# A decoder layer with sixteen experts on one core: the fifth product of the experts' output with 128 rows, and another place for the first expert's up products

## The chip, the core and the metric

The program runs on one core of one Trainium2 chip. A core has a tensor engine (PE; its weight loads are listed apart as PEld), a vector engine (DVE), a scalar engine (ACT), GpSimd (POOL), and SyncE (SP), which here only issues transfers. Each engine works through its own instructions in a fixed order and waits at an instruction until the semaphores named in it have been reached. The metric is the device time of one execution in microseconds (us); lower is better.

## The reference

The layer is: layer norm, self-attention with 4-bit weights, layer norm, cross-attention over a compressed context, layer norm, and a mixture of 16 experts, each part added to `x`. Tokens: 16 x 64 = 1024 of width 256. Only the experts matter for this change:

```
scores = softmax(xt @ Wg.T)                      # 1024 x 16
...                                              # top 4 of the 16, limited to 2 of 4 groups
h = silu(einsum('td,eid->eti', xt, W1)) * einsum('td,eid->eti', xt, W3)   # inner width 176
expert_out = einsum('eti,edi->etd', h, W2)
y = einsum('etd,te->td', expert_out, combine)
z = (silu(xt @ Ws1.T) * (xt @ Ws3.T)) @ Ws2.T    # shared expert, width 352
return y + z
```

## The kernel before

**Precision.** The products of the experts are done in `fp32r`, a format coarser than float32. To keep accuracy each operand is split into a high part (a rounded copy, made on ACT) and a low part (what the rounding left, a subtraction on DVE or POOL); `parts_of` (L111) does it for activations and `weight_parts` (L268) for an expert's weights. A product is then high by high, high by low, and low by high: three matmuls in place of one.

**An expert's inner width is 176 = 128 + 48.** The first 128 make one block of `h` with its high part `h_p[0]` and low part `h_p[1]`. The other 48 (filled up with zeros to 64) make a second block. Its high and its low part share one tile, `h_p[2]`: rows 0 to 63 hold the high part, rows 64 to 127 the low part. The second block of the down weights, `w2[1]`, has the same 64 rows twice, once in each half. So one matmul of 128 rows, `(h[2], w2[1][0])`, gives high by high and low by high at once. What remains of that block is high by the weights' low part, `(h[2][:64], w2[1][1][:64])`, a matmul of 64 rows. `expert_output` (L291) is thus five matmuls into one stretch of PSUM, of which the fifth has 64 rows.

**Who calls it.** `send_outputs` (L1273) calls it three times for each of the 15 routed experts (384 slots in three blocks of 128). `dense_out` (L1098) and `dense_output` (L1321) call it for the sixteenth expert, which is computed for all tokens: four times each.

**The routed experts.** Each token's rows are scattered by POOL's indirect transfers into `xd`, a table in device memory with 384 slots for each expert (`send`, L820; a token's k-th choice is sent with the k-th round of sends). `expert_inputs` (L1233) loads an expert's 384 rows (`xr`, issued by SP; the load waits for the rounds of sends that may hold rows of it), turns them with six PE transposes, and splits them (`xs`). `expert_weights` (L1222) loads its weights (640 KB, issued by SP), rounds them on ACT (L270) and subtracts on DVE, or on DVE and POOL (L275). `expert_hidden` (L1255) does 18 up matmuls into three PSUM tiles, then silu, product and splitting on ACT and DVE; it leaves its last up matmul in `up_done[0]`. `send_outputs` does the three times five down matmuls, copies the results out of PSUM (L1281) and scatters them back with three indirect transfers (L1286). At the end `load_outputs` fetches them and `add_outputs` (L1309) adds them with their weights.

**Order.** The loop at L1335 works on three experts at a time: in step `e` it asks for the inputs and weights of expert `e`, the hidden part of expert `e-1`, and the outputs of expert `e-2`. The text of the program does not give the order alone: a scheduler in the framework orders the instructions of each engine by its own estimate, and `tc.issue_after(ins)` tells it to place what follows behind an instruction. In step 2 the hidden part of expert 1 comes ahead of the inputs of expert 2, which are placed behind `up_done[0]`; in all other steps inputs come first. The raw weights (`w`) have two buffers, their parts three, `xr` three.

Of the kernel before, what the change touches and what calls it, by code (L numbers as in the profile page):

```python
# [42 lines left out]
E, INTER, NGRP, TOPK, TOPKG = 16, 176, 4, 4, 2  # L43
# [28 lines left out]
def decoder_layer(ctx: ExitStack, tc: tile.TileContext, a: dict, out: bass.AP):  # L72
# [29 lines left out]
    def matmuls(ps, pairs):  # L102
        for n, (l, r) in enumerate(pairs):
            m = nc.tensor.matmul(ps, lhsT=l, rhs=r, start=(n == 0), stop=(n == len(pairs) - 1))  # L104
        return m.ins
# [184 lines left out]

    def expert_output(ps, w, h_p, cols):  # L291

        w2 = [[p[:, W_UP + k * D : W_UP + (k + 1) * D] for p in w] for k in range(2)]
        h = [p[:, cols] for p in h_p]
        return matmuls(
            ps,
            [
                (h[0], w2[0][0]),
                (h[0], w2[0][1]),
                (h[1], w2[0][0]),  # L300
                (h[2], w2[1][0]),
                (h[2][:64], w2[1][1][:64]),
            ],
        )

    with ExitStack() as attn:
# [528 lines left out]
        def slots_are_short():  # L835

            ps = av_tile()[:, :E]
            nc.tensor.matmul(ps, lhsT=ones, rhs=before[:, NI, :], start=True, stop=True)
            most = fs.tile([128, 1], F32, tag="most", name="most")
            nc.vector.tensor_reduce(most, ps[:, : E - 1], AX.X, ALU.max)  # L840
            short = fs.tile([128, 1], I32, tag="short", name="short")
            nc.vector.tensor_scalar(short, most, SLOTS + 0.5, None, ALU.is_gt)
            return nc.values_load(short[:1], min_val=0, max_val=1)
# [98 lines left out]
        with (  # L942
# [155 lines left out]
            def dense_out(h_p, half, tiles, add):  # L1098
                for k in tiles:
                    ps = av_tile()[:, :D]  # L1100
                    expert_output(ps, w_last, h_p, slice(k * 128, k * 128 + 128))
                    add(half, k, ps)
# [117 lines left out]
    gated, up_done = [None], [None]  # L1220

    def expert_weights(src, down_lo=nc.gpsimd):  # L1222
        return weight_parts(
            src,
            fw.tile([128, W_COLS], F32, tag="w123", name="w123"),
            [
                fw.tile([128, W_COLS], F32R, tag=f"w123{n}", name=f"w123{n}", bufs=3)
                for n in range(2)
            ],
            down_lo,  # L1230
        )

    def expert_inputs(e):  # L1233

        t = fx.tile([128, SLOTS // 128, ROW], F32, tag="xr", name="xr", bufs=3)
        first = TOPK * NT + (E - 2 - e) * SLOTS
        load = nc.sync.dma_start(
            out=t, in_=xd[first : first + SLOTS].rearrange("(b p) d -> p b d", p=128)
        ).ins
        for k in range(min(TOPK, e + 1)):  # L1240
            behind(load, sent_for[k])
        to = fx.tile([128, SLOTS // 128], U32, tag="to", name="to", bufs=4)
        parts = [fx.tile([128, 2, SLOTS], F32R, tag=f"xs{n}", name=f"xs{n}") for n in range(2)]
        for c in range(2):
            ps = at_tile([128, 512])[:, :SLOTS]
            for b in range(SLOTS // 128):
                nc.tensor.transpose(
                    ps[:, b * 128 : (b + 1) * 128], t[:, b, c * 128 : (c + 1) * 128], ident
                )
            lows.append(parts_of(ps, parts[0][:, c, :], parts[1][:, c, :]))  # L1250
        with tc.issue_after(lows[-1]):
            nc.vector.tensor_copy(to, t[:, :, D + e])
        return parts, to

    def expert_hidden(w, xs, n):  # L1255


        ps, up_done[0] = expert_up(w, xs, n)
        g, h, g2, h2 = (
            fh.tile([128, SLOTS], F32, tag=tag, name=tag)[:, :n] for tag in ("g", "h", "g2", "h2")  # L1260
        )
        h_p = [
            fh.tile([128, SLOTS], F32R, tag=tag, name=tag)[:, :n] for tag in ("hp0", "hp1", "hp2")
        ]
        nc.scalar.activation(g, ps[0], AF.Silu)
        nc.vector.tensor_tensor(h, ps[1], g, ALU.mult)
        parts_of(h, h_p[0], h_p[1])
        silus.append(nc.scalar.activation(g2[64:], ps[2][:64], AF.Silu).ins)
        nc.vector.tensor_tensor(h2[:64], ps[2][64:], g2[64:], ALU.mult)
        gated[0] = parts_of(h2[:64], h_p[2][:64], h_p[2][64:])  # L1270
        return h_p

    def send_outputs(e, w, h_p, to):  # L1273
        last = []
        y = fy.tile([128, SLOTS // 128, D], F32, tag="y", name="y")
        ps = [av_tile() for _ in range(2)]
        for b in range(SLOTS // 128):
            cols = slice(b * 128, (b + 1) * 128)
            last.append(expert_output(ps[b // 2][:, b % 2 * D : (b % 2 + 1) * D], w, h_p, cols))
            last.append(  # L1280
                (nc.vector.tensor_copy if b == 1 and e < E - 3 else nc.scalar.copy)(  # L1281
                    y[:, b, :], ps[b // 2][:, b % 2 * D : (b % 2 + 1) * D]
                ).ins
            )
        for b in range(SLOTS // 128):
            sent = nc.gpsimd.indirect_dma_start(  # L1286
                out=yd[: (E - 1) * SLOTS + min(TOPK, E - 1 - e) * NT],
                out_offset=bass.IndirectOffsetOnAxis(ap=to[:, b : b + 1], axis=0),
                in_=y[:, b, :],
                in_offset=None,  # L1290
            ).ins
            side_by_side(sent, returned)
            last.append(sent)
        return last

    def load_outputs(k):

        tiles = []
        for n in range(NI // 2):
            t = fy.tile([128, 2, D], F32, tag="got", name="got", bufs=9)  # L1300
            first = (E - 1) * SLOTS + (TOPK - 1 - k) * NT + n * 256
            got = nc.sync.dma_start(
                out=t, in_=yd[first : first + 256].rearrange("(i p) d -> p i d", p=128)
            ).ins
            behind(got, returned)
            tiles.append(t)
        return tiles
# [10 lines left out]
    def dense_hidden(w, half, n):  # L1318
        return expert_hidden(w, [p[:, :, n * 256 : n * 256 + 256] for p in normed[half]], 256)

    def dense_output(w, h_p, half, n, add):  # L1321
        for b in range(2):
            ps = av_tile()[:, :D]
            expert_output(ps, w, h_p, slice(b * 128, b * 128 + 128))
            add(half, 2 * n + b, ps)
# [7 lines left out]
    with tc.issue_after(lows[-1]), tc.issue_after(silus[-1]):  # L1333
        ws[0] = expert_weights(a["W123"][0], nc.vector)
    for e in range(E + 1):  # L1335
        if e == 2:

            low = lows[-1]
            hs[e - 1] = expert_hidden(ws[e - 1], xs[e - 1][0], SLOTS)
        if e < E - 1:  # L1340
            low = lows[-1]
            with tc.issue_after(up_done[0] if e == 2 else low):
                xs[e] = expert_inputs(e)
            if e >= 1:
                with tc.issue_after(low), tc.issue_after(silus[-1]):
                    ws[e] = expert_weights(a["W123"][e], nc.vector if e < 3 else nc.gpsimd)
        if 0 <= e - 1 < E - 1 and e != 2:
            hs[e - 1] = expert_hidden(ws[e - 1], xs[e - 1][0], SLOTS)
        if e - 2 >= 0:
            if e == E:  # L1350

                with tc.issue_after(gated[0]):
                    h_p = dense_hidden(w_last, 1, 0)
            last = send_outputs(e - 2, ws.pop(e - 2), hs.pop(e - 2), xs.pop(e - 2)[1])
            if e - 2 == E - TOPK - 2:
                short = slots_are_short()
            if e == 6:
                with tc.issue_after(gated[0]), tc.issue_after(silus[-1]):
                    routed.append(weights_of_choices(1))
            k = e - 2 - (E - 1 - TOPK)  # L1360
            if k >= 0:
                got[k] = load_outputs(k)
# [135 lines left out]
```

## Time and profile before

| what | value |
|---|---|
| median of 3 runs | 598.12 us (594.16, 598.12, 598.73) |
| the profiled execution | 594.01 us, span from first to last instruction 592.2 us |
| mean granted PE clock | 0.973 |
| self-attention and the start | 0 to about 220 us |
| cross-attention and routing | about 220 to 459 us |
| routed experts | about 459 to 574 us |
| last additions and stores | about 574 to 592 us |

A group line of the profile reads: line, engine, operation, output<-input, rows*columns of the array that are used, the shape, the count; then busy time and the mean duration of one in ns; then idle time before it, and what ended the idle time. The duration of a matmul includes the depth of the pipeline: matmuls overlap, so what one costs the engine is the distance from its start to the start of the next. In the timeline like instructions in a row are merged into one line, with the start of the first, the length of all, and their number. The windows view gives each engine's busy time in a stretch, the granted PE clock (1.00 is full), and the share of time in which the DMA engines were busy.

### The profile page before, as it was taken

To read this page: it belongs to the slowest core of one execution; us is meant where nothing else is said; L and a number is where in the kernel's file an instruction comes from. 1 tells how busy PE (TensorE), PEld (TensorE's weight loads), DVE (VectorE), ACT (ScalarE), POOL (GpSimd) and SP (SyncE) were. 2 spreads that over 40 slices of the span, in tenths; PEclk is the share of its full clock that TensorE was granted. 3 is DMA by queue.
4 is the path that set the end of the run, shared out by engine and by line. 5 is a ranking of instruction groups with operands and counts; after the bars stand their busy time and mean duration, and the time that the engine had idled before them with its cause. 6 is when DMAs were issued, how large, how long until landed. Compare 5 with 4: busy or idle time off the path is not lost.

```text
span 592.2 us, 10572 instructions
## 1 busy us (share of the span) xinstructions
PE 558.4 (94%) x3999; PEld 452.9 (76%) x3999; DVE 403.4 (68%) x879; ACT 280.6 (47%) x524; POOL 232.5 (39%) x213
## 2 busy tenths in 40 slices
PE   5989999999999989999999999999989799999992
PEld 5878988988889875757777577576778688888871
DVE  5454636554465789847668487789648587888766
ACT  3657574575665432221431332333435276867551
POOL 4192000010000004526334454442545546768773
PEclk8989999999999999999999999999989799999996
DMA  8667042141300499481020000000413677565275
GB/s 247 159 195 208 25 136 91 53 143 50 95 1 1 137 265 293 128 243 30 1 70 1 8 1 1 28 2 26 165 69 95 231 225 239 176 228 184 100 252 184
DMA packets 56293, 70.82 MB, mean 120 GB/s; under 512 B 13872, under 2 KB 42768, under 8 KB 56240
## 3 DMA queue, kind: packets, MB, share of 16 engines
q1 hardware_dynamic: 51408, 58.71, 33.5%
q0 software_dynamic: 3696, 10.36, 4.6%
q10 hardware_dynamic: 1136, 1.05, 0.5%
q8 instruction: 32, 0.52, 0.4%
q14 instruction: 21, 0.17, 0.1%
HBM read 48.61 MB, written 21.86 MB: 119 GB/s over the span
## 4 chain that ended last, share of the span: by engine, by line


## 5 line engine op out<-in xcount | busy, mean ns | idle before, releaser
L973 POOL TENSOR_TENSOR roped<-rt,rt 128x512 f32<-128x512 f32 x48 | 62.7, 1328 | 82.8 <-DVE rt L967 80.5
L967 DVE TENSOR_TENSOR rt<-mm,rope_q 128x512 f32<-128x512 f32 x96 | 61.5, 684 | 23.7 <-PE mm L104 23.1
L104 PE MATMUL mm<-xn,w_q 128*128 128x512 f32 x288 | 74.2, 403 | 0.5 <-ACT xn L214 0.5
L104 PEld LDWEIGHTS mm<-xn,w_q 128*128 128x128 f32 x288 | 52.1, 188 | 14.4 <-issue 2.7
L1286 POOL DMA_INDIRECT yd<-y,to x45 | 49.4, 1099 | 34.7 <-DVE y L1281 13.5
L104 PE MATMUL mm<-xs,w 128*128 128x384 f32 x270 | 57.0, 358 | 1.2 <-ACT w L270 0.6
L104 PEld LDWEIGHTS mm<-xs,w 128*128 128x128 f32 x270 | 48.0, 196 | 4.4 <-DVE w L275 0.8
L318 ACT ACTIVATE p<-p 128x512 f32<-128x512 f32 x32 | 20.2, 630 | 65.7 <-DVE p L317 65.7
L513 POOL TENSOR_TENSOR wo<-code,scale 128x512 fp32r<-128x512 f32 x8 | 10.6, 1330 | 102.1 <-PE mm L104 94.1
L988 PE MATMUL mm<-roped,w_s 128*64 128x512 f32 x192 | 46.3, 601 | 0.0
L104 PE MATMUL av<-w,hp 128*128 128x256 f32 (+1 forms) x225 | 45.8, 314 | 0.1
L605 DVE TENSOR_TENSOR x<-mm,x 128x256 f32<-128x256 f32 x64 | 26.0, 419 | 29.1 <-PE mm L104 27.9
L104 PEld LDWEIGHTS av<-w,hp 128*128 128x128 f32 (+1 forms) x225 | 33.9, 187 | 9.0 <-issue 0.7
L104 PE MATMUL mm<-wo,o 128*128 128x256 f32 x256 | 39.5, 295 | 0.1
L104 PE MATMUL mm<-wv,xn 128*128 128x256 f32 x256 | 36.0, 292 | 1.4 <-ACT kT L550 1.4
L315 DVE TENSOR_REDUCE sm_m<-at 128x8 f32<-128x512 f32 x32 | 21.7, 679 | 21.8 <-PE at L565 20.9
L104 PE MATMUL mm<-xn,wq 128*128 128x512 f32 x128 | 35.4, 413 | 0.4 <-ACT xn L214 0.4
L104 PE MATMUL mm<-xn,wk 128*128 128x512 f32 x128 | 35.4, 407 | 0.0
L582 PE MATMUL av<-pt,v 128*128 128x128 f32 x256 | 34.5, 277 | 0.0
L104 PEld LDWEIGHTS mm<-wv,xn 128*128 128x128 f32 x256 | 32.5, 193 | 2.5 <-ACT kT L550 1.6
L104 PEld LDWEIGHTS mm<-wo,o 128*128 128x128 f32 x256 | 32.9, 190 | 1.5 <-issue 0.4
L582 PEld LDWEIGHTS av<-pt,v 128*128 128x128 f32 x256 | 32.0, 191 | 1.2
(216 smaller groups left out, 1150.1 us busy)
## 6 DMA issues: line engine op xcount, KB each, us to landing
w<-in_W SPq DMA_DIRECT2D x15, 640.0 KB
code<-in_codes SPq DMA_DIRECT2D x32, 256.0 KB
scale<-in_scales SPq DMA_DIRECT2D x32, 256.0 KB
xr<-xd SPq DMA_DIRECT2D x15, 408.0 KB
xd<-zeros SPq DMA_DIRECT2D x8, 720.0 KB
yd<-zeros SPq DMA_DIRECT2D x8, 512.0 KB
got<-yd SPq DMA_DIRECT2D x16, 256.0 KB
wq<-in_Wq SPq DMA_DIRECT2D x4, 512.0 KB
```

Source lines behind the costliest of these rows:

```text
L104: m = nc.tensor.matmul(ps, lhsT=l, rhs=r, start=(n == 0), stop=(n == len(pairs) - 1))
L315: nc.vector.tensor_reduce(m, sc, AX.X, ALU.max)
L318: exps.append(nc.scalar.activation(p, p, AF.Exp, scale=scale).ins)
L513: mults[n] = eng.tensor_tensor(w, *loaded[gr].pop(n), ALU.mult).ins
L582: nc.tensor.matmul(av[:, k * 128 : (k + 1) * 128], lhsT=v[:, i, k0 : k0 + HD], rhs=pt[:, i].rearrange("p a q -> p (a q)"), start=True, sto ...
L605: nc.vector.tensor_tensor(x[i], ps, x[i], ALU.add)
L967: nc.vector.tensor_tensor(mt, ps3, rope_table(t, 2 * ab + k), ALU.mult)
L973: nc.gpsimd.tensor_tensor(r.rearrange("p (b s) -> p b s", s=S), one, two, op)
L988: nc.tensor.matmul(ps[h // 2][(h % 2) * 64 : (h % 2) * 64 + 64], lhsT=w_s[:, t, blk, ab, :], rhs=roped[2 * t + ab], start=first[h], stop=l ...
L1286: sent = nc.gpsimd.indirect_dma_start(out=yd[: (E - 1) * SLOTS + min(TOPK, E - 1 - e) * NT], out_offset=bass.IndirectOffsetOnAxis(ap=to[:, ...
```

## The change

Two edits. In `expert_output` the fifth matmul takes all 128 rows of `h_p[2]` and of the weights' low part; with it the product of low by low, which was left out before, comes in for the second block. In the loop the arrangement of step 2 is used in step 1 as well: the hidden part of expert 0 comes ahead of the inputs of expert 1, which are placed behind its last up matmul, and ahead of the weights of expert 1.

```diff
@@ expert_output
                 (h[0], w2[0][1]),
                 (h[1], w2[0][0]),
                 (h[2], w2[1][0]),
-                (h[2][:64], w2[1][1][:64]),
+                (h[2], w2[1][1]),
@@ the loop over the experts
     for e in range(E + 1):
-        if e == 2:
+        if e in (1, 2):
             low = lows[-1]
             hs[e - 1] = expert_hidden(ws[e - 1], xs[e - 1][0], SLOTS)
         if e < E - 1:
             low = lows[-1]
-            with tc.issue_after(up_done[0] if e == 2 else low):
+            with tc.issue_after(up_done[0] if e in (1, 2) else low):
                 xs[e] = expert_inputs(e)
...
-        if 0 <= e - 1 < E - 1 and e != 2:
+        if 0 <= e - 1 < E - 1 and e > 2:
             hs[e - 1] = expert_hidden(ws[e - 1], xs[e - 1][0], SLOTS)
```

In the built program this moves instructions on four engines between the end of the shared expert and the first outputs of expert 1. PE does the 18 up matmuls of expert 0 without a break; before, the six transposes of expert 1 stood after the third and the twelfth of them. On ACT the rounding of expert 1's weights (L270) comes behind the two silus of expert 0 instead of ahead of the shared expert's last pieces; on DVE the two subtractions for those weights come behind the two products (L1266, L1269) of expert 0. On SP the first three loads (`xr` of experts 0 and 1, weights of expert 2) stay; the weights of expert 3 are asked for behind `xr` of experts 2 and 3 instead of ahead of them. POOL's order stays as it was. Two of the four output blocks in `dense_out` also come 10 matmuls or so later on PE.

## The prediction

> **What bounds the kernel now.** I read the page first (which engine is full), then the groups by shape for the stretch from 380 us on, then PE's timeline to see single starts, then the windows for clock and load, and last the queues of SP and POOL. The view of the chain of waits holds nothing for this run, so what ends last is read from PE's own gaps. The page, and the windows of the expert stage:
>
> ```profile
> PE 558.4 (94%) x3999; PEld 452.9 (76%) x3999; DVE 403.4 (68%) x879; ACT 280.6 (47%) x524; POOL 232.5 (39%) x213
> ...
> 474.00:574.00 100.00, 98.89 (x578) 85.70 (x578) 80.23 (x150) 67.30 (x137) 67.29 (x57) 1.00 0.61 200
> ```
>
> From 474 to 574 us (columns PE, PEld, DVE, ACT, POOL, clock, DMA share, GB/s) PE has work at all times but 1.1 us; DVE is busy 80 us, ACT and POOL 67. So PE's pitch sets this stage, with DVE next. The groups by shape:
>
> ```profile
> L104 PE MATMUL av<-w,hp 128*128 128x256 f32 x180 | 32.9, 297 | 0.1
> L104 PE MATMUL av<-w,hp 64*128 64x256 f32 x45 | 17.2, 381 | 0.0
> L104 PE MATMUL mm<-ws,sh 96*128 96x256 f32 x24 | 3.8, 281 | 0.0
> ```
>
> The 45 fifth products (64 rows) last 381 ns each, their 128-row neighbours 297, products of the same width with 96 rows 281. Durations overlap, so I take starts. The timeline, asked from later and later points inside one group of five (a merged line starts with the first matmul still running):
>
> ```profile
> 487.38 0.94 PE L104 MATMUL av<-w,hp 128*128 128x256 f32 x5
> ...
> 487.50 0.83 PE L104 MATMUL av<-w,hp 128*128 128x256 f32 x4
> ...
> 487.62 0.71 PE L104 MATMUL av<-w,hp 128*128 128x256 f32 x3
> ...
> 487.73 0.59 PE L104 MATMUL av<-w,hp 128*128 128x256 f32 x2
> ...
> 487.94 0.38 PE L104 MATMUL av<-w,hp 64*128 64x256 f32 x1
> 488.25 0.97 PE L104 MATMUL mm<-xs,w 128*128 128x384 f32 x4
> ```
>
> The first four start 0.12 us apart, the 64-row one 0.21 after its forerunner, and the next instruction 0.31 after it. The group takes 488.25 - 487.38 = 0.87 us where five steps of 0.117 would be 0.585: 0.285 us too much. The start of the stage:
>
> ```profile
> 456.35 3.38 PE L104 MATMUL mm<-ws,sh 128*128 128x256 f32 x27
> ...
> 460.63 0.79 PE L104 MATMUL mm<-xs,w 128*128 128x384 f32 x3 [0.24 <-ACT xs L112]
> 465.50 0.87 PE L1247 MATMUL at<-ident,xr 128*128 128x128 f32 x3 [4.09 <-DMA xr<-xd]
> 466.03 3.23 PE L104 MATMUL mm<-xs,w 128*128 128x384 f32 x9
> ...
> 455.20 6.38 SPq L1237 DMA_DIRECT2D xr<-xd  x2
> 461.74 2.34 SPq L269 DMA_DIRECT2D w<-in_W  x2
> 470.25 4.21 SPq L1237 DMA_DIRECT2D xr<-xd  x3
> ...
> 468.00:469.00 1.00, 1.00 (x4) 0.96 (x4) 0.00 (x0) 0.00 (x0) 0.94 (x1) 0.50 1.01 411
> ```
>
> PE stands 4.09 us at expert 1's transposes until its rows land, and then runs at clock 0.50: windows of 1 us show 0.50 from 465 to 471 and 0.75 in 471 to 472. The nine products at 466.03 need 3.02 us (469.05 - 466.03), 0.335 each; at full clock 18 of them need 3.25 (546.87 to 550.12), 0.18 each.
>
> **The change part by part. (a) The fifth product.** It occurs 15 x 3 = 45 times in the routed experts and 4 + 4 times for the sixteenth. Each saves 0.285 us of PE if it then steps like its 128-row neighbours: 12.8 us for the 45. The bounds: 0 and 0.285 each. Against it stands the Trainium skill, "TensorE: Matmul & The Clock Gate", Part 3 and "Why this matters for your kernels": a single matmul of 32 rows takes the same time as one of 128, so rows below 128 gain by concurrency alone. By that rule 64 or 128 rows are one price and (a) is worth nothing. The rows decide: the shared expert mixes 96-row and 128-row products, and 27 of them start (3.38 - 0.28) / 26 = 0.119 us apart, so neither fewer rows nor the end of a group costs; only the 64-row kind does, on both its sides. I take 0.285. By the rule the sum below would lose its larger term.
>
> What of the 12.8 lies on the path: from 474 to 574 PE would need 87 us, DVE still 80, and POOL 67 plus 45 gaps of 0.30 that follow its indirect transfers, 81. They hide nothing now (they have 20 us to spare), but after the saving they have 7 and will make PE wait at times. One row prices that: in 510 to 530 us DVE is busy 17.13 of 20 and PE loses 0.9 of 20. At DVE 92% I allow 3% to 4% of 87 us, 3.2 us. So (a) brings 9.6 there, between 4 (DVE and POOL take most) and 12.8. The four blocks of `dense_out` lie ahead of the wait for expert 1's rows, which they only lengthen; the four at the end lie beside DVE's additions (PE waits 1.3 to 1.7 us for DVE there): nothing for both. If DVE were faster those at the end would bring 1.1.
>
> **(b) Expert 0's up products ahead of expert 1's rows.** Moved forward: 18 matmuls, two silus, two roundings, four DVE operations. Put behind them: six transposes, two roundings, two subtractions and the slot copy of expert 1, and the rounding (1.26 us) and two subtractions (1.55) of its weights. The wait itself stays: expert 1's load keeps its place on SP, second of these, behind the same sends, and lands at about 465.5. But 15 of the 18 products now run inside it: from 461.4, held a little by DVE's low parts (ready at about 462.1), to about 464.2. That takes 15 x 0.18 = 2.7 us out of the time after 465.5. PE then stands only 1.3 us (2.4 with the four shorter `dense_out` blocks ahead).
>
> The clock: 465.5 to about 471.5 ran at half, so 3.0 us of work were lost. The skill's page on the clock gate (Part 1, "What's actually happening") says the clock falls after one idle window of about 3.4 us and that windows run freely. By it a stand of 1.3 to 2.4 us leaves the clock at 1.00 and (b) brings 2.7 + 3.0 = 5.7; without it, if any stand of over a microsecond lowered the clock, 2.7. The nearest rows (a stand of 4.09 fell, stands under 0.6 us in 474 to 574 did not) leave it open; I take the full clock.
>
> Given back: ACT rounds expert 1's weights after the second silu, at about 464.6 to 465.9, so DVE's chain from there is 1.55 (weights) + 0.5 + 0.56 + 0.5 + 0.16 + 0.56 = 3.8, until about 469.7; the 18 up products of expert 1 then end at about 470.4 instead of 474.7, a gain of 4.3. Next late: `xr` of expert 3 waits for the last round of sends (POOL ends it at 470.2) and lands at about 474.5, where PE now wants it at about 474; and the weights of expert 3 are queued on SP behind that load. They were issued at 463.7; now at about 472.5, land 2 to 4 us later (640 KB at the 300 GB/s that the DMA engines reach there) and need 1.26 us on ACT: 477 to 478, where PE wants them at about 477.5. That is 0 to 1 us. Less DMA traffic at 464 to 469 (share 1.0 now) helps expert 1's and 2's rows by as much again at best. I take 4.0 for (b), between 0.5 (clock falls, late weights) and 6.
>
> **Sum.** 594.0 - 9.6 - 4.0 = 580.4 for an execution like the profiled one. It lies 4.1 under the median of the runs shown, which by the same sum goes to 584.5. I say 583, since I can't tell which kind of run will be in the middle.
>
> **The rivals.** *DVE and POOL become the bound.* For: 80 and 81 us of work in a stage of 87, with chains between them; a DVE operation of 0.56 us lasts far longer beside POOL's subtraction:
>
> ```profile
> 539.41 1.95 DVE L113 TENSOR_TENSOR hp<-h,hp 128x384 fp32r<-128x384 f32 x1
> ...
> 539.64 1.29 POOL L275 TENSOR_TENSOR w<-w,w 128x512 fp32r<-128x512 f32 x1
> ```
>
> Against: DVE idles 20 of 100 us now. Then (a) brings 4 to 5 and (b) 3: about 590 on the median.
>
> *The price is not of the 64 rows* but of whatever stands fifth. Against: the 96-row groups above close without it, and the price falls on both sides. Then (b) alone: about 594.
>
> *Slower: more collisions of DVE with POOL.* An expert takes 6.73 us now (up products at 540.13 and 546.87), DVE about 5.5 of it. A collision like the one shown adds 1.4. A tighter PE moves DVE's splitting under POOL's subtraction more often. Two more per expert would make DVE need 8.3 and cost 15 x 1.6 = 24, less 4 from (b): about 618; it decides from 1.2 + 0.3 = 1.5 us more per expert on. Against: the subtraction runs once per expert, 1.3 to 2.0 us long, and one collision per expert is there already.
>
> **How the numbers follow.** What a measurement of this kernel can tell from no change is about 1%, 6 us. Chances: the forecast 0.71 (576 to 590), DVE and POOL as the bound 0.18 (587 to 594, four fifths of it faster by over 1%), the price elsewhere 0.07 (592 to 597), slower 0.04. Faster 0.71 + 0.14 + 0.01 = 0.86, same 0.10, slower 0.04. Range: from 575 (594.0 with all of 12.8 and 6) to 592, which takes in most of the first rival.
>
> **What would show it.** No 64*128 row is left; the fifth product starts 0.12 after the fourth and the next 0.12 to 0.18 after it; an expert's pitch falls from 6.73 to 6.0 to 6.2; DVE's share from 474 on rises to about 90%. PE's wait for expert 1's rows is under 2.5 us, and no 0.50 shows after 464 us. The prediction is wrong if a 128-row fifth product keeps the 0.3 us behind it, if the pitch stays above 6.5 with PE waiting for DVE or POOL, or if a new PE wait of over 2 us stands ahead of expert 2's transposes or expert 3's first product.

## The result, and the profile after

The changed kernel takes 589.94 us, the kernel before 594.30 (medians of 18 runs each, 586.70 to 593.14 and 590.03 to 598.73): a ratio of 0.992, 95% interval 0.9895 to 0.9944. About 4.4 us came, where the prediction had 13.6. The profiled execution took 590.21 us, with a span of 588.4 and a mean granted clock of 0.979. Ratios here and below leave out executions more than 1.5% slower than the fastest of their kernel (a single one of 1042 us, of the kernel with 128 rows only, among them), while the medians take in all. From L293 on, line numbers are higher by one than before.

The page's row of busy time, and the window from 474 to 574 us (columns PE, PEld, DVE, ACT, POOL, clock, DMA share, GB/s), of the changed kernel:

```profile
PE 540.4 (92%) x3999; PEld 444.3 (76%) x3999; DVE 401.0 (68%) x879; ACT 279.4 (47%) x524; POOL 230.1 (39%) x213
...
474.00:574.00 100.00, 83.94 (x567) 79.78 (x566) 80.10 (x152) 64.50 (x134) 70.88 (x60) 1.00 0.66 217
```

PE was busy 98.89 of these 100 us before and is busy 83.94 now. Not all of this is saved work: the routed products now end 6.5 us sooner, and the window takes in a stand of 4.89 us behind them (the last line below). What became of the saving shows in the steady experts further down. The group of down products, and the timeline around one group of five:

```profile
L104 PE MATMUL av<-w,hp 128*128 128x256 f32 x225 | 35.1, 289 | 4.0 <-DVE y L1282 3.3 <-DVE most L841 0.5 <-ACT y L1282 0.3
...
505.84 0.75 PE L104 MATMUL av<-w,hp 128*128 128x256 f32 x5
506.43 0.49 PE L1248 MATMUL at<-ident,xr 128*128 128x128 f32 x3
...
573.75 0.77 PE L104 MATMUL av<-w_last,hp 128*128 128x256 f32 x2 [4.89 <-DVE x L936]
```

All 225 products now have 128 rows, and five of them with what follows take 506.43 - 505.84 = 0.59 us, where it was 0.87. At its source the saving is what the prediction said. The end of the group line shows a first price: PE waits 3.3 us for DVE's copy `y` out of PSUM, where these products had 0.1 us of idle time in all before.

To compare kernels I cut the steady part out: from the first up product of expert 5 to that of expert 13, eight experts. It runs from 498.20 to 553.90 us before and from 496.20 to 549.30 after. The windows of the two kernels, in this order:

```profile
498.20:553.90 55.70, 54.68 (x315) 47.37 (x314) 46.77 (x89) 38.70 (x76) 39.62 (x32) 1.00 0.61 200
```

```profile
496.20:549.30 53.10, 47.27 (x317) 45.08 (x316) 46.99 (x90) 38.75 (x78) 41.10 (x34) 1.00 0.67 221
```

PE's busy time falls by 7.4 us, 0.93 an expert; the time by 2.6, 0.33 an expert. DVE is busy for the same 47 us in both, which is now 88% of the time. What PE waits for in the same windows, before and then after (us in total, times, longest):

```profile
PE mm L104 <- ACT w L270: 0.6, 1, 0.6
PE mm L104 <- DVE w L275: 0.2, 1, 0.2
```

```profile
PE mm L104 <- ACT w L270: 2.8, 4, 1.4
PE mm L104 <- DVE w L275: 1.7, 2, 1.3
PE av L104 <- DVE y L1282: 0.8, 1, 0.8
PE av L104 <- DVE most L841: 0.5, 1, 0.5
```

0.8 us of waiting became 5.8. So two thirds of what was saved on PE turned into standing. The largest part, 2.8 us, is for ACT's rounding of the weights. The copy `y` has only 0.8 here; 2.46 of its 3.3 us fall in one wait at the start of the stage (shown further down). ACT's rounding itself waits 0.5 us in this window, for PE, and never for a load, so the loads of weights don't hold these experts. How such a wait comes about shows in the timeline of the changed kernel:

```profile
514.62 1.68 DVE L1253 CAST to<-xr 128x3 uint32<-128x3 f32 x1
514.98 1.28 POOL L275 TENSOR_TENSOR w<-w,w 128x512 fp32r<-128x512 f32 x1
516.21 0.41 DVE L1282 COPY y<-av 128x256 f32<-128x256 f32 x1
516.68 0.85 PE L104 MATMUL av<-w,hp 128*128 128x256 f32 x5 [0.84 <-DVE y L1282]
516.87 0.94 DVE L275 TENSOR_TENSOR w<-w,w 128x768 fp32r<-128x768 f32 x1
517.87 1.66 PE L104 MATMUL mm<-xs,w 128*128 128x384 f32 x8 [0.34 <-DVE w L275]
518.32 1.10 ACT L112 CAST hp<-h 128x384 fp32r<-128x384 f32 x2 [2.31 <-DVE h L1267]
```

DVE's copy of 3 slot numbers a row takes 0.16 us elsewhere. Here it lasts 1.68 and ends at 516.30, with POOL's subtraction (514.98 + 1.28 = 516.26). Behind it in DVE's queue stand `y`, which PE wants for the next down products, DVE's part of the weights, which PE wants for the next up products, and `h`, which ACT stands 2.31 us for.

### The profile page after: what moved, and what is told of

The parts are those of the page before. It is cut to its first block, busy times and chain, and to the rows that moved or that the text cites. A ratio compares the mean times of both kernels' runs of the same rounds, so it can differ in the third digit from the quotient of the medians.

```text
span 588.4 us, 10571 instructions
## 1 busy us (share of the span) xinstructions
PE 540.4 (92%) x3999; PEld 444.3 (76%) x3999; DVE 401.0 (68%) x879; ACT 279.4 (47%) x524; POOL 230.1 (39%) x213
## 4 chain that ended last, share of the span: by engine, by line
PE 71%; DVE 12%; DMA 6%; ACT 4%; issue 4%; POOL 2%; SPq 0%; DVEq 0%; ACTq 0%; POOLq 0%
PE mm L104 42%; PE mm L989 6%; PE av L583 5%; PE at L566 4%; DMA yd<-y,to 4%; PE at L335 3%; PE at L1012 2%; PE av L1025 2%; PE av L104 2%; PE mm L431 2%; ACT w L270 2%; DVE rt L968 1%; DVE w L275 1%; DMA w<-in_W 1%; DVE x L1317 1%
## 5 line engine op out<-in xcount | busy, mean ns | idle before, releaser
L104 PE MATMUL mm<-xs,w 128*128 128x384 f32 x270 | 54.5, 344 | 8.3 <-ACT w L270 3.2
L104 PEld LDWEIGHTS mm<-xs,w 128*128 128x128 f32 x270 | 45.8, 188 | 11.5 <-ACT w L270 4.2
L104 PE MATMUL av<-w,hp 128*128 128x256 f32 x225 | 35.1, 289 | 4.0 <-DVE y L1282 3.3
L104 PEld LDWEIGHTS av<-w,hp 128*128 128x128 f32 x225 | 30.5, 188 | 5.7 <-DVE y L1282 3.9
```

## The experiments

A series is a set of runs of several kernels on one chip, with the kernel before among them; "again" in the table is another series. "First sends" below is the first of POOL's last sixteen scatters of rows (448.05 us in the profile before; sixteen others, of the first half of the tokens, go out from 411.67 on). It is the reference point because it moves by itself: up to it all these kernels run the same instructions in the same order, and yet it came between 445.28 and 453.86 us in their profiles. "Expert n" is its first up product after that, "end" the end of the span after that; the pitch is from expert 4 to expert 14, divided by ten. All are read from the timelines, one profile a row. A pitch says little of a kernel whose expert 4 comes early and whose expert 5 does not.

| kernel | ratio to before (95%) | expert 0 | expert 1 | expert 4 | pitch | end |
|---|---|---|---|---|---|---|
| before | 1 | 12.6 | 23.5 | 43.5 | 6.85 | 144.2 |
| changed | 0.992 (0.9895 to 0.9944) | 11.6 | 18.1 | 43.3 | 6.48 | 141.1 |
| changed, again | 0.9908 (0.9883 to 0.9934) | 11.6 | 18.1 | 43.0 | 6.49 | 140.4 |
| 128 rows only | 0.996 (0.9938 to 0.9982) | 15.8 | 22.5 | 43.2 | 6.48 | 140.5 |
| 128 rows only, again | 0.9892 (0.9856 to 0.9928) | 11.8 | 22.0 | 41.2 | 6.54 | 139.4 |
| reordering only | 1.0187 (1.0146 to 1.0229) | 22.1 | 29.2 | 50.9 | 6.86 | 152.5 |
| reordering only, again | 0.9994 (0.9977 to 1.0011) | 12.5 | 19.0 | 41.5 | 6.85 | 142.2 |
| reordering only, third | 0.9992 (0.9974 to 1.0011) | 12.5 | 19.1 | 42.8 | 6.85 | 143.9 |
| before, low parts on DVE | 0.9932 (0.9908 to 0.9955) | 12.6 | 22.3 | 43.1 | 6.68 | 142.3 |
| 128 rows, low parts on DVE | 0.9803 (0.976 to 0.9846) | 11.6 | 22.5 | 40.5 | 6.25 | 134.8 |
| the same, again | 0.9827 (0.9788 to 0.9866) | 11.6 | 22.4 | 40.5 | 6.03 | 132.4 |
| changed, low parts on DVE | 0.9841 (0.9773 to 0.991) | 15.1 | 22.6 | 42.3 | 6.04 | 135.4 |
| the same, again | 0.9824 (0.9784 to 0.9865) | 11.8 | 18.0 | 38.2 | 6.21 | 132.1 |
| changed, weights of 1 early | 0.9998 (0.9971 to 1.0025) | 15.2 | 24.9 | 46.8 | 6.60 | 147.3 |
| the same, again | 0.9921 (0.9885 to 0.9956) | 11.6 | 17.5 | 40.4 | 6.48 | 138.3 |

**The parts alone.** The kernel before with the 128-row product, where no instruction changes its place on any engine:

```
-                (h[2][:64], w2[1][1][:64]),
+                (h[2], w2[1][1]),
```

> The kernel before with only the fifth product at 128 rows; every engine keeps its order. Theory A (VectorE is the next bound): each group of five takes 0.59 us instead of 0.87, but an expert's pitch from 500 us on falls by only about 0.3 us and VectorE has almost no idle time there: ratio 0.990 to 0.996 (3 to 6 us). Rival B (the fifth product alone brings what the sum said, 9 us or more, and the reordering takes it back): ratio 0.985 or less.

593.67 us, 0.996: the upper edge of the first theory. On another chip:

> The kernel before with the 128-row fifth product alone, once more. Theory A (the steady experts lose 0.375 us each, some 4 us over ten experts and 5 with the others, of which the end gives 1 back; the first runs fell on a chip where the start of the stage was late): ratio 0.989 to 0.994, pitch 6.47 to 6.48 us. Rival B (it is worth no more than the first runs said): 0.994 to 0.998.

586.49 us against 593.18 of the kernel before on that chip, 0.9892. That chip also ran the changed kernel again (below) at 589.03. So the gain of the change is in this one line, and no gain of the reordering on top of it shows. The two series differ by more in whole times (gains of 2.6 and 6.7 us) than from the first sends to the end of the span (140.5 and 139.4 us, against 144.2 before and 141.1 and 140.4 for the changed kernel). The reordering in the kernel before:

```
-        if e == 2:
+        if e in (1, 2):
...
-            with tc.issue_after(up_done[0] if e == 2 else low):
+            with tc.issue_after(up_done[0] if e in (1, 2) else low):
...
-        if 0 <= e - 1 < E - 1 and e != 2:
+        if 0 <= e - 1 < E - 1 and e > 2:
```

> The kernel before with only the reordering of step 1; the fifth product keeps 64 rows. Theory A: the stand for expert 1's rows shrinks, but the weights of expert 3 are loaded late and ScalarE stands for them about 4 to 5 us, so expert 4's up products start within 1 us of before: ratio 0.997 to 1.002. Rival B: the reordering costs more than it brings: ratio 1.005 or more. Rival C: it brings the 4 us of the sum: 0.993 or less.

606.91 us, a loss of 11: the first rival's case. The table says where: expert 0 starts 22.1 us after the first sends, where before it was 12.6, and after that nothing is lost. Ahead of expert 0 the edit changes no more than the order of a few groups of the shared expert and of `dense_out`, and the rounding and subtraction of weights between them. Windows of this run:

```profile
464.00:468.00 4.00, 1.03 (x8) 0.83 (x8) 0.43 (x2) 0.00 (x0) 2.90 (x4) 1.00 0.59 164
468.00:472.00 4.00, 2.39 (x10) 1.99 (x10) 2.61 (x5) 0.00 (x0) 3.27 (x3) 0.61 0.57 193
472.00:476.00 4.00, 0.00 (x0) 0.00 (x1) 1.53 (x5) 0.48 (x1) 2.82 (x3) 0.50 0.91 333
...
475.47 0.48 ACT L112 CAST xs<-at 128x384 fp32r<-128x384 f32 x1 [13.45 <-remote]
```

PE, DVE and ACT all stand while POOL's sends go on at their usual step, and the profile names no instruction that ACT's wait of 13.45 us ended with. So I ran it again:

> The kernel before with the reordering alone, once more. Theory A (the loss of 10 us in the first runs came from where TensorE stood still at the start of the stage, and belongs to that kernel's own timing): ratio 1.012 to 1.024 again, expert 0's first up product 20 us or more after the first rows sent by GpSimd, pitch from expert 4 to 14 as before the change, 6.8 to 6.9 us. Rival B (it was an accident of those executions): ratio 0.990 to 1.003, expert 0's first product 12 to 16 us after the first rows sent.

> The kernel before with the reordering alone, a third time. Theory A (what it gains at expert 1, 4.5 us, is given back by expert 4, because the rows and weights that the first four experts need come no sooner): ratio 0.996 to 1.001, pitch 6.85 us. Rival B (the loss of the first runs is usual): 1.010 or more. Rival C (it is worth the 4 us of the prediction): 0.991 to 0.995.

592.96 and 592.80 us, 0.9994 and 0.9992, with expert 0 at 12.5. The second theory of the one and the first of the other hold: the loss did not come back, though its interval of 1.0146 to 1.0229 seemed to exclude that. It goes with the series and its chip, not with the edit alone: all four kernels of that series (128 rows only, reordering only, and the first runs of two edits below, low parts on DVE and weights of 1 early) started expert 0 15.1 us or more after the first sends, the other fourteen profiles 11.6 to 12.6. In whole times the reordering alone is worth 0.3 to 0.4 us, which is nothing. What it does is in the table: expert 1 comes 4.4 us sooner, expert 4 only 0.7 to 2.0, and the end 0.3 to 2.0. The changed kernel once more, beside these:

> The changed kernel as it is, once more, beside the others on the same chip. Theory A (the start of the expert stage differs from one chip or execution to the next by some us, through TensorE's clock and what it stands still, and the steady pitch does not): ratio 0.988 to 0.997, and from expert 4 to expert 14 again 6.4 to 6.5 us each, wherever expert 0 starts. Rival B (the pitch of 6.48 was an accident of one execution): a pitch outside 6.35 to 6.6.

589.03 us, 0.9908, pitch 6.49, and the same starts to within 0.3 us. The pitches are no accident: from expert 4 on, the two profiles of the changed kernel agree within 0.07 us at each expert.

**GpSimd's subtraction.** DVE makes the low parts of all down weights, a DVE operation of 0.69 us more per expert from expert 3 on, and POOL's is gone:

```
-ws[e] = expert_weights(a["W123"][e], nc.vector if e < 3 else nc.gpsimd)
+ws[e] = expert_weights(a["W123"][e], nc.vector)
```

> The changed kernel with the low part of the down weights made by VectorE for all experts (GpSimd makes it from expert 3 on in the changed kernel). Theory A1 (VectorE is the bound, and what fills it is its operations being held by GpSimd's subtraction, about 1.1 us per expert): 0.6 us of work more, 1.1 us of holding less per expert, so about 5 us faster than the changed kernel, ratio 0.981 to 0.987, and no VectorE operation of 384 columns over 1 us. Theory A2 (VectorE's own amount of work is the bound): 12 times 0.6 us slower, ratio 1.000 to 1.005. If VectorE is no bound: 0.990 to 0.994.

592.00 us, 0.9841, with runs that scatter from 582.69 to 599.73 us and a wide interval, and on the other chip:

> The same with the reordering, once more. Theory A (the reordering is worth nothing): within 0.004 of the kernel without it, either way. Rival C (it is worth the 4 us of the prediction): lower than that kernel's ratio by 0.005 to 0.009. Rival B (it costs): higher by more than 0.005.

583.88 us, 0.9824. With more to do, DVE is busy less. Its groups in eight steady experts of the changed kernel, and then of this one (the last two numbers ahead of the second bar are busy us and mean ns of one):

```profile
L113 DVE TENSOR_TENSOR hp<-h,hp 128x384 fp32r<-128x384 f32 x9 | 7.8, 867 | 0.2
L113 DVE TENSOR_TENSOR hp<-h,hp 64x384 fp32r<-64x384 f32 x8 | 5.6, 706 | 0.3
```

```profile
L113 DVE TENSOR_TENSOR hp<-h,hp 128x384 fp32r<-128x384 f32 x9 | 5.0, 553 | 0.2
L113 DVE TENSOR_TENSOR hp<-h,hp 64x384 fp32r<-64x384 f32 x8 | 4.4, 552 | 0.2
L275 DVE TENSOR_TENSOR w<-w,w 128x512 fp32r<-128x512 f32 x8 | 5.5, 690 | 0.0
```

Both subtractions go back to one duration, and what PE waits for in these eight experts falls from 5.8 to 2.0 us:

```profile
PE at L1248 <- DVE xs L113: 1.1, 1, 1.1
PE mm L104 <- ACT w L270: 0.6, 1, 0.6
PE av L104 <- ACT y L1282: 0.3, 1, 0.3
```

The edit takes away two things at once: the hold on DVE, and 1.3 to 2.05 us an expert of POOL's own queue ahead of its scatters. PE waits for POOL itself in neither window, but no run here parts the two. The same edit in the kernel before:

> The kernel before, with VectorE making the low parts of every expert's second weights (512 of 1280 columns move from GpSimd to VectorE from expert 3 on). Nothing else is changed; the 64-row fifth products stay. Theory A (TensorE bounds an expert before the change at about 6.7 to 6.8 us, and VectorE, held by GpSimd's subtraction, becomes the bound only once the five products have got shorter): TensorE has little to gain, the pitch from expert 4 to expert 14 goes from 6.86 to 6.7-6.8 us, ratio to the kernel before 0.995 to 1.002. Rival B (the two costs simply add, whichever engine bounds): the pitch falls by the 0.44 us that the same edit took from the changed kernel (6.48 to 6.04), ratio 0.990 to 0.994.

589.67 us, 0.9932: the time falls into the second theory's range. The pitch falls by 0.17 to 6.68, which is the first one's figure. Neither theory has both. With the 128-row product, and no reordering:

> The kernel before, with the 128-row fifth product and with VectorE making all the low parts of the second weights, without the reordering. Theory A: pitch from expert 4 to expert 14 about 6.0 to 6.1 us against 6.86 before and 6.47 with the 128-row product alone; ratio to the kernel before 0.980 to 0.988. On the reordering: if it brings 2 to 4 us, as the prediction had it, this kernel is slower than the changed kernel with the same move (0.984) by 0.003 to 0.007; if it costs as much as it brings or more, it is as fast or faster (0.975 to 0.984).

> The 128-row product and all low parts on VectorE, without the reordering, once more. Theory A: ratio 0.976 to 0.985 as in the first runs, pitch 6.0 to 6.1 us where the clock stays full.

583.12 and 583.30 us, 0.9803 and 0.9827. (In the first profile the clock fell to half for 3.4 us near 524; hence its pitch of 6.25.) This version beats both kernels, and the reordering makes no difference to it (0.9824 and 0.9827 on one chip). The eight steady experts with the low parts on DVE, in the kernel before and then with 128 rows (second series), neither with the reordering:

```profile
495.10:549.10 54.00, 54.00 (x316) 47.50 (x315) 44.07 (x97) 38.30 (x77) 23.67 (x24) 1.00 0.62 203
```

```profile
496.20:545.20 49.00, 46.69 (x315) 45.20 (x315) 44.21 (x97) 37.79 (x77) 24.87 (x24) 1.00 0.70 224
```

Here the 128-row product takes (54.0 - 49.0) / 8 = 0.63 us from an expert, with POOL's subtraction only 0.33. In the whole time this is not seen: 589.67 to 583.30 is 6.4 us with the low parts on DVE, 593.18 to 586.49 is 6.7 with them on POOL, each uncertain by about 3. From the first sends to the end of the span it is 142.3 - 132.4 = 9.9 us with the low parts on DVE (7.5 in the profile with the lowered clock) and 3.7 to 4.8 with them on POOL. So the interplay is shown for the stage, by one or two profiles each; in the whole time, which takes in what moves ahead of the first sends, it is not.

**Is it DVE's queue alone?** All three result copies go to ACT:

```
-(nc.vector.tensor_copy if b == 1 and e < E - 3 else nc.scalar.copy)(
+nc.scalar.copy(
```

> The changed kernel with all three copies of an expert's result on ACT: one copy of 0.42 us leaves VectorE per expert, GpSimd keeps its subtraction. Theory A (VectorE's queue bounds the steady experts of the changed kernel): the pitch from expert 4 to 14 falls from 6.48 by 0.2 to 0.42 us, ratio 0.984 to 0.989. Rival B (it is GpSimd's chain of subtraction and scatters that bounds): pitch 6.4 to 6.5, ratio 0.989 to 0.994. Rival C (ACT becomes the bound, or delays the scatters): pitch over 6.5, ratio over 0.994.

591.22 us, 0.9945, pitch 6.73: the third case by its numbers, but not clearly. Expert 4 comes 3.6 us sooner than in the changed kernel and expert 5 only 0.9, and this makes the pitch long; from expert 5 to 13 it takes 52.0 us, the changed kernel 53.1. The end comes at 141.0, as in the changed kernel. PE now waits 3.8 us in eight experts for ACT's rounding of the weights, one us more than in the changed kernel. So the copy's place in DVE's queue is not the whole bound: what left DVE came back in good part as waiting for ACT. That DVE, ACT and POOL hold each other in a ring fits this, but is argued from the waits.

**The weights that came late.** The expected small price of the reordering was that expert 3's weights are issued later. To undo that, expert 1's weights are rounded sooner, so that the load goes out ahead of the later experts' rows:

```
+        silu = silus[-1]
...
-                with tc.issue_after(low), tc.issue_after(silus[-1]):
+                with tc.issue_after(low), tc.issue_after(silu if e == 1 else silus[-1]):
```

> The changed kernel with expert 1's weights rounded early, as before the change; so the weights of expert 3 are loaded ahead of the rows of experts 2 and 3 again. Theory A (the late weights of expert 3 gave the start back): ScalarE's stand of 4.8 us for a weights transfer is gone, expert 4's up products start 3 to 4 us earlier than in the changed kernel: ratio 0.984 to 0.988. Rival (the wait for the first scattered outputs near 489 us sets the start in any order): same as the changed kernel, 0.990 to 0.994.

595.76 us, 0.9998, with expert 0 already 3.6 us later than in the changed kernel and ACT's wait again ended by nothing that the profile names. It tells nothing of the weights. Again:

> The changed kernel with the next weights' rounding at expert 1 released by the silu before (so that the load of expert 3's weights goes out on SyncE ahead of the later experts' rows, as in the kernel before), once more. Theory A (the late weights cost the changed kernel about 5 us between expert 2's and expert 4's first up products, and the first runs of this edit hid it behind TensorE standing at the start): expert 2 to expert 4 in 13 to 15 us instead of 18, and ratio 0.980 to 0.988. Rival B (rounding expert 1's weights so early puts ACT and VectorE in front of the first experts' own work, and gives it back): expert 0 and expert 1 start 2 us or more later after the first rows sent than in the changed kernel (11.6 and 18.1), ratio 0.990 to 1.002.

589.40 us, 0.9921: ACT's stand for a load of weights is gone, and from expert 2 to expert 4 it takes 12.4 us instead of 18.1, as the first theory had it, but expert 2 comes 2.7 us later. What PE waits for between 460 and 490 us of this run:

```profile
PE at L1248 <- DMA xr<-xd: 4.8, 2, 4.1
```

The rows of expert 2 are now behind the weights. One wait has taken the other's place in part: expert 4 still starts at 40.4, 2.9 us ahead of the changed kernel, at the same pitch, and the end comes at 138.3 instead of 140.4 to 141.1. So the late weights did cost some 2 to 3 us there; the whole time can't tell this (0.9885 to 0.9956). Neither case as written holds. With the other edits:

> The changed kernel with both edits: VectorE makes all the low parts of the second weights, and expert 1's weights are rounded early. Theory A: the two gains add, pitch from expert 4 to 14 about 6.05 us and expert 4 two or more us earlier after the first rows sent (41 or less): ratio 0.972 to 0.980. Rival B (early rounding brings nothing): ratio 0.980 to 0.988, like the changed kernel with the first edit alone (0.984).

> The changed kernel with all three edits (low parts on VectorE, expert 1's weights early, result copies on ACT). Theory A (VectorE still sets the pace at 6.05 us, with TensorE's own starts adding up to about 5.4): pitch 5.7 to 5.9, ratio 0.966 to 0.976. Rival B (at 6.05 the pace is TensorE's and the chain through ACT): pitch 6.0 or more, ratio as without the third edit or up to 0.005 higher.

585.08 us, 0.9847 (0.9814 to 0.988), pitch 5.97, expert 4 at 41.4, and 584.12 us, 0.9853 (0.9816 to 0.9891), pitch 6.28, expert 4 at 38.4. The rival of each holds: no gain over low parts on DVE alone shows.

## Why the prediction was wrong, by its steps

**The fifth product costs 0.285 us more than it should: right.** The group went from 0.87 to 0.59 us. The rule of the Trainium skill ("TensorE: Matmul & The Clock Gate", "Why this matters for your kernels") that few rows take the time of many would have made this edit worth nothing; the runs have 64 rows among 128-row products cost more than 128.

**The allowance for DVE and POOL, 3.2 of 12.8 us: the first term that failed.** It was taken from one stretch in which PE lost 0.9 us of 20 with DVE 17 us busy. That is 4.5% at a DVE share of 86%, and yet 3% to 4% was taken for a share of 92%. And 0.6 of the 0.9 us was a wait for ACT's rounding of the weights (the line in the waits of before), not for a full DVE. A busy share cannot say how late the operations are that PE waits for. The waits in eight experts grew by 5.0 us, 0.62 an expert, and over 15 that is 9.4 of the 12.8. What stays by the windows is 15 x 0.33 = 4.9 us; the kernel with this edit alone gained 6.7 and 2.6 in two series. The first rival (DVE and POOL become the bound, (a) brings 4 to 5) named the place, the size of (a) and most of the mechanism, and showed POOL beside a stretched DVE operation as its evidence; ACT's rounding, the longest of PE's waits, it did not name. That its time of about 590 was met is in part luck: it was reckoned from the median of 598.12 with 3 us for (b), and the kernel before then ran at 594.30 and (b) brought nothing. It was given 0.18. Argued against it was that DVE idles 20 of 100 us. It still does; what counts is when its operations come, not how much time is free between them. The sign named for being wrong here, a pitch above 6.5 with PE waiting for DVE or POOL, was met over the eight experts (53.1 / 8 = 6.64) and just missed from expert 4 on (6.48). Without POOL's subtraction the saving is (54.0 - 49.0) / 8 = 0.63 us an expert, 9.4 over 15, close to the forecast 9.6: the allowance had the size of a kernel in which POOL makes no low parts.

**The reordering, 4.0 us: the second term that failed, and all of it.** Expert 1's gain was put at 4.3 us and is 4.4 (5.4 in the changed kernel). Also right: PE's wait for expert 1's rows fell from 4.09 to 0.98 us, and the clock stayed at 1.00. That was not safe by the length of the stand, though: in the third run of the reordering alone no stand was over 1.58 us, and the clock still fell to half from 468.27 to 471.68 (last section). The term "0 to 1 us" for what comes late next was wrong. In the changed kernel:

```profile
464.14 0.85 PE L1248 MATMUL at<-ident,xr 128*128 128x128 f32 x6 [0.98 <-DMA xr<-xd]
460.00:474.00 14.00, 10.48 (x61) 9.06 (x62) 8.49 (x17) 7.89 (x16) 6.96 (x8) 1.00 0.67 206
...
472.69 0.35 SPq L269 DMA_DIRECT2D w<-in_W  x1
...
479.04 1.26 ACT L270 CAST w<-w 128x1280 fp32r<-128x1280 f32 x1 [4.77 <-DMA w<-in_W]
480.38 2.05 POOL L275 TENSOR_TENSOR w<-w,w 128x512 fp32r<-128x512 f32 x1 [4.28 <-ACT w L270]
488.91 0.17 DVE L1253 CAST to<-xr 128x3 uint32<-128x3 f32 x1 [3.13 <-DMA yd<-y,to]
489.96 0.86 PE L104 MATMUL av<-w,hp 128*128 128x256 f32 x5 [2.46 <-DVE y L1282]
```

The load is issued at 472.69, as forecast (472.5). It landed after 6.3 us instead of 2 to 4. And the forecast asked only when PE wants these weights. ACT's rounding stands at a fixed place in its queue: ACT stood there 4.77 us, DVE and POOL behind it, POOL's later scatters behind its subtraction, and DVE's slot copy and `y` behind a scatter, until PE stood 2.46 us, some ten us later, for a copy out of PSUM. Expert 2 to expert 4 took 18.1 us in the changed kernel, 13.2 with the 128-row product alone (again); against that kernel the changed one is 3.9 us ahead at expert 1 and 2.1 behind at expert 4.

The 3.0 us for the clock were no gain on the path either. With the 128-row product alone the clock fell as before:

```profile
459.00:466.00 7.00, 3.80 (x14) 3.73 (x15) 1.67 (x3) 0.48 (x1) 5.48 (x6) 0.52 0.96 323
```

and its expert 4 still started 41.2 us after the first sends, 2.1 us ahead of the changed kernel with its full clock. The first experts are fed by POOL's last sixteen sends, 1.26 us or more each, and by the loads behind them on SP; these runs fit the reading that PE working sooner between two deliveries moves no delivery.

**The tail, costed at nothing: a smaller miss.** The last routed down product started 6.5 us sooner (571.78 to 565.24), the last scatter 4.9 (573.88 to 569.00), the end of the span 3.8. POOL's last scatters follow each other at 1.26 to 1.6 us from 562.20 on, and DVE then waits for fetched results. That cost 2.7 us.

**The slower rival** (a tighter PE brings two collisions more per expert, 1.5 us and up) did not come: DVE's busy time in eight experts went from 46.77 to 46.99. The rival "price elsewhere" fell with the group of 0.59 us.

Open: why three engines stood at the start in the runs of one series; whether DVE's hold or POOL's own queue makes most of what its subtraction costs; and why the parts' gains in steady experts and in whole times don't agree better than to some 3 us.

## What to carry to other kernels

When the fullest engine gets less to do, don't take an allowance from the busy share of the next one: list which of its operations the first will wait for, and what in its queue, or on an engine that holds it, comes ahead of them. Where work is fed by deliveries (sends, rows, weights on one queue), moving compute forward is worth nothing unless the next delivery moves too, and a load issued later is charged at the place where a queue first stands for it, not where its data is at last used. A gain at the start of a stage counts only when it is still there some steps on; and a single series of runs with a tight interval can be 2% off for the same kernel.

## What was not expected of the hardware

POOL's subtraction of 512 columns (1.28 us) held a DVE copy of 3 columns for 1.68 us instead of 0.16. Between 460 and 575 us of the changed kernel all eleven DVE operations that last over 0.25 us more than the shortest of their kind (where there are four or more of a kind) overlap an elementwise operation of POOL. The operations that read PSUM beside it (`xs<-at`, `h<-mm`, `y<-av`) keep their duration (the 16 of `xs<-at` in eight experts last 555 ns on average, and 554 in the kernel without POOL's subtraction). And where DVE's own subtraction started 0.05 us ahead of POOL's, as at 502.57, it was POOL's that took 2.05 us instead of 1.3. An operation of 0.69 us more on DVE made DVE 2.7 to 2.8 us less busy in eight experts once POOL's was gone (46.77 to 44.07 in the kernel before, 46.99 to 44.20 in the changed one).

A stand of PE, DVE and ACT together, with the DMA engines 57% to 91% busy, went with 606.91 us for a kernel that took 592.80 to 592.96 in two other series; the profile names no instruction of this core that ended it.

Ahead of the first sends, where all kernels are alike, the clock stood at half for 10 us in some executions and for 3.4 or not at all in others, and the first sends came up to 8.6 us apart. From POOL's very first scatter (411.67 before) to these sends it takes 34.3 us in the three profiles with no half clock between, 35.5 to 36.4 in the ten with 3.4 us of it, and 38.7 to 39.8 in the five with 10.2. So up to 5.5 us go with the clock there; what is left was there before (the first scatter itself came between 409.7 and 415.3 us).

What the clock went by shows when all 18 profiles are cut, from 25 to 570 us, into steps of 3.41 us, laid by the start of a stretch of half clock (these stretches last 3.41, 6.83 or 10.24 us there). Taken are the steps at full clock. After each of the 45 in which PE was busy less than 45.5% of the time, the next step ran at half; after none of the 2729 with 55% or more; and after 6 of the 18 between. So no long stand was needed: in the third run of the reordering alone PE was busy 39% of the step from 464.86 to 468.27, with 1.58 us as its longest stand. This is a count over these profiles, not a rule tested by an edit.

Back to the start of the stage: these are windows of the kernel with the 128-row product alone in its two series:

```profile
440.00:443.00 3.00, 3.00 (x15) 3.00 (x16) 0.00 (x0) 0.37 (x1) 2.39 (x3) 0.50 0.37 132
```

```profile
440.00:443.00 3.00, 3.00 (x16) 2.46 (x15) 2.83 (x26) 1.83 (x4) 0.00 (x0) 1.00 0.00 0
```

The one has its first sends at 453.42, the other at 445.35. Two profiles are therefore compared from a point inside the stage, and the whole times only as medians.
